# The masks of a dense attention: from matmuls in the sum of scores to transposed masks that multiply the exponentials

## The chip, the cores and the metric

The kernel runs on one core of one Trainium2 chip. The metric is the device time of one execution in microseconds (us), taken without the profiler; a profile of one further execution stands beside it. Times of the kernel before: 1467.72, 1467.99 and 1475.14 us, median 1467.99 us.

## The reference, cut to what matters

Two layers follow one another, each a graph attention and a mixture of experts, on 2708 nodes with 256 features. The change touches the first attention alone. The second attention uses the same adjacency matrix.

```python
# x: (2708, 256) float32; adj: (2708, 2708) int32, zeros and ones
def _L0_gnn_ref(x, adj, Wq, bq, Wk, bk, Wv, bv):
    q = x @ Wq.T + bq
    k = x @ Wk.T + bk
    v = x @ Wv.T + bv
    scores = q @ k.T / jnp.sqrt(jnp.asarray(d, q.dtype))      # d = 256
    neg = jnp.asarray(-9000000000000000.0, scores.dtype)
    scores = jnp.where(adj > 0, scores, neg)
    attention = jax.nn.softmax(scores, axis=-1)
    return jax.nn.elu(attention @ v)
...
x = x + _L0_gnn_ref(_layernorm(x, axis=-1), adj, ...)
x = x + _L0_ffn_ref(_layernorm(x, axis=-1)[None], ...)[0]     # 8 experts, top 2, hidden 1024
x = x + _L1_gnn_ref(_layernorm(x, axis=-1), adj, ...)         # masked by adj too
x = x + _L1_ffn_ref(_layernorm(x, axis=-1)[None], ...)[0]     # 8 experts, top 2, hidden 512
```

A weight of a masked pair is zero after the softmax. So it is the same to push its score far down before the exponential or to multiply its exponential by zero after it.

## The kernel before

Queries go in blocks of 512 (five full blocks and one of 148), keys in 22 tiles of 128 (`NT = 22`; the last has 20 rows). For each block and each key tile `k` there is one step: `scores` makes the sums with the keys on the partitions and the queries along the row, then exponentials `p`; `attend` multiplies `p` of two steps earlier (`LAG = 2`) with `v` into accumulators that live for the whole block.

Rows of `adj` have the queries on the partitions, so a mask lies the wrong way round for the sums. The kernel before turns it with TensorE: `apart` holds 1 where there is no edge, and a matmul of `apart` with -32768 times the identity adds -32768 to the sums of masked pairs. VectorE then reads the mask, turned, back from the sums (`mT`), and each block's `mT` is written to device memory (`neighbours`), from where the second attention takes it.

```python
def load_mask(b, i, into):                       # one of four column quarters of a block's adj
    q = N // 4                                   # 677
    for j, t in enumerate(BLOCKS[b][2]):         # the block's tiles of 128 queries
        r = ROWS[t]
        adj = wide.tile([P, q], I32, name="adj", bufs=4)
        nc.sync.dma_start(adj[:r], a["adj"][t * P : t * P + r, i * q : (i + 1) * q])
        nc.vector.tensor_scalar(
            into[:r, j, i * q : (i + 1) * q], adj[:r], 0, None, ALU.is_le, saturate=False,
        )                                                                    # L255
        yield
...
def scores(b, k, g, apart, mT):
    b0, nb, ts_ = BLOCKS[b]
    kr, k0 = ROWS[k], k * P
    ps = ps_s.tile([P, BN], F32, name="s")                                   # two buffers
    for c in range(DC):                                                      # DC = 2
        nc.tensor.matmul(ps[:kr, :nb], xnT[:, c, k0 : k0 + kr], g[:, c, :nb],
                         start=(c == 0), stop=False)                         # L339
    for j, t in enumerate(ts_):
        r = ROWS[t]
        nc.tensor.matmul(ps[:kr, j * P : j * P + r], apart[:, j, k0 : k0 + kr],
                         minus_big[:, :r], start=False, stop=(j == len(ts_) - 1))   # L345
    p = of_block(b, "p", [P, nb], F32, bufs=4)
    nc.scalar.activation(p[:kr, :nb], ps[:kr, :nb], AF.Exp, scale=1.0 / 16.0)       # L350
    nc.vector.tensor_scalar(mT[:kr, k, :], ps[:kr, :nb], -BIG / 2, None, ALU.is_gt,
                            saturate=False)                                  # L351
    return p

def attend(b, k, p, accs):
    kr = ROWS[k]
    for j, t in enumerate(BLOCKS[b][2]):
        r = ROWS[t]
        nc.tensor.matmul(accs[j][:r], p[:kr, j * P : j * P + r], v[:kr, k, :],
                         start=(k == 0), stop=(k == NT - 1))                 # L361
...
for b, (b0, nb, ts_) in enumerate(BLOCKS):
    mT = of_block(b, "mT", [P, NT, nb], FP8)
    ...
        later_mask = (x for i in range(4) for x in load_mask(b + 1, i, apart_next))
    for k in range(NT):
        ...                                      # block 0: x tiles, its own masks, prepare()
        late.append((b, k, scores(b, k, g, apart, mT)))
        if len(late) > LAG:
            b_, k_, p = late.pop(0)
            ...
            attend(b_, k_, p, accs)
        ...
        if k >= 2:
            next(later_mask, None)               # one piece of the next block's mask per step
        if b > 0:
            if k % 5 == 1 and background:
                background.pop(0)()              # pack one expert's weights, DRAM to DRAM (L587 ...)
            line.step()                          # routing of finished query tiles (L666 ... L731)
        ...
    nc.sync.dma_start(neighbours[b][:], mT)      # L441
```

`adj`, `apart`, `p` and `mT` come from pools with a fixed number of buffers (4 for `adj` and `p`, 2 for `apart` and `mT`). The order of instructions on SyncE's queue is that of the program; it issues the loads, the packing of weights and the stores of the routing.

Of the kernel before, what the change touches and what calls it, by code (L numbers as in the profile page):

```python
# [10 lines left out]
I32 = mybir.dt.int32  # L11
FP8 = mybir.dt.float8e4
U32 = mybir.dt.uint32
BF16 = mybir.dt.bfloat16
AF = mybir.ActivationFunctionType
ALU = mybir.AluOpType
# [3 lines left out]
P = 128  # L20
N = 2708
D = 256
DC = D // P
# [3 lines left out]
NT = (N + P - 1) // P  # L27
# [6 lines left out]
GROUP = 4  # L34
BIG = 32768.0
LAG = 2
# [17 lines left out]
def adj_ffn_kernel(ctx: ExitStack, tc: tile.TileContext, a: dict, out: bass.AP):  # L54
    nc = tc.nc
# [14 lines left out]
    nc.gpsimd.memset(minus_half, -0.5)  # L70

    minus_big = const.tile([P, P], BF16, name="minus_big")
    nc.vector.tensor_scalar(minus_big, ident, -BIG, None, ALU.mult)

# [147 lines left out]
    def layer0_attention(line):  # L222
        with ExitStack() as scope, ExitStack() as until_last:
# [18 lines left out]
            def load_x(t):  # L242
                xin[t] = rows.tile([P, D], F32, name="xin", bufs=9)
                nc.sync.dma_start(xin[t][: ROWS[t]], a["x"][t * P : t * P + ROWS[t], :])

            def load_mask(b, i, into):

                q = N // 4
                for j, t in enumerate(BLOCKS[b][2]):
                    r = ROWS[t]  # L250
                    adj = wide.tile([P, q], I32, name="adj", bufs=4)
                    nc.sync.dma_start(
                        adj[:r], a["adj"][t * P : t * P + r, i * q : (i + 1) * q]
                    )
                    nc.vector.tensor_scalar(  # L255
                        into[:r, j, i * q : (i + 1) * q], adj[:r], 0, None, ALU.is_le,
                        saturate=False,
                    )
                    yield

            def mask_of(b):
                n = len(BLOCKS[b][2])
                apart = of_block(b, "apart", [P, n, N], FP8)
                for j, t in enumerate(BLOCKS[b][2]):
                    if ROWS[t] < P:
                        nc.gpsimd.memset(apart[:, j, :], 0.0)
                return apart

# [3 lines left out]
            with tc.tile_pool(name="fold", bufs=1, side="right") as fold:  # L272
                wq = load_dmajor(fold, "L0_gnn_Wq", D)
                wk = load_dmajor(fold, "L0_gnn_Wk", D)
                apart = mask_of(0)
                for _ in load_mask(0, 0, apart):
                    pass
# [55 lines left out]

            def scores(b, k, g, apart, mT):
                b0, nb, ts_ = BLOCKS[b]
                kr, k0 = ROWS[k], k * P
                ps = ps_s.tile([P, BN], F32, name="s")
                for c in range(DC):
                    nc.tensor.matmul(  # L339
                        ps[:kr, :nb], xnT[:, c, k0 : k0 + kr], g[:, c, :nb],  # L340
                        start=(c == 0), stop=False,
                    )
                for j, t in enumerate(ts_):
                    r = ROWS[t]
                    nc.tensor.matmul(  # L345
                        ps[:kr, j * P : j * P + r], apart[:, j, k0 : k0 + kr], minus_big[:, :r],
                        start=False, stop=(j == len(ts_) - 1),
                    )
                p = of_block(b, "p", [P, nb], F32, bufs=4)
                nc.scalar.activation(p[:kr, :nb], ps[:kr, :nb], AF.Exp, scale=1.0 / 16.0)  # L350
                nc.vector.tensor_scalar(  # L351
                    mT[:kr, k, :], ps[:kr, :nb], -BIG / 2, None, ALU.is_gt,
                    saturate=False,
                )
                return p
# [39 lines left out]
            for b, (b0, nb, ts_) in enumerate(BLOCKS):  # L395
                mT = of_block(b, "mT", [P, NT, nb], FP8)
                nc.gpsimd.memset(mT[:, NT - 1, :], 0.0)
                later_mask = iter(())
                if b + 1 < len(BLOCKS):
                    apart_next = mask_of(b + 1)  # L400
                    later_mask = (x for i in range(4) for x in load_mask(b + 1, i, apart_next))
                for k in range(NT):
                    if b == 0:
                        if k + 6 < NT:
                            load_x(k + 6)
                        if k % 5 == 0 and k < 15:
                            for _ in load_mask(0, k // 5 + 1, apart):
                                pass
                        if k + 4 < NT:
                            prepare(k + 4)  # L410

                    j = k - (2 if b == last else NT - 1 - GROUP)
                    if 0 <= j < len(ts_):
                        load_x(ts_[j])
                    late.append((b, k, scores(b, k, g, apart, mT)))
                    if len(late) > LAG:
# [22 lines left out]
                    if b == last and k == LAG + 2:  # L439
                        experts0.begin()  # L440
                nc.sync.dma_start(neighbours[b][:], mT)  # L441
                if b < last:
                    for _ in later_mask:
                        pass
                    g, apart = g_next, apart_next
            for b_, k_, p in late:
# [536 lines left out]
    for xd in (xd0, xd1):  # L983
        nc.sync.dma_start(xd[N:, :], nobody[:, :D])

    neighbours = [
        dram.tile([P, NT, nb], FP8, name=f"neighbours{b}") for b, (_, nb, _) in enumerate(BLOCKS)
    ]
    line = Line(3)
    layer0_attention(line)  # L990
    with tc.tile_pool(name="mask", bufs=1) as mp:
        mTs = [
            mp.tile([P, NT, nb], FP8, name=f"mT{b}") for b, (_, nb, _) in enumerate(BLOCKS)
        ]
# [45 lines left out]
```

## Time and profile before

| | |
|---|---|
| median time | 1467.99 us |
| span of the profiled execution | 1466.9 us |
| TensorE matmul busy | 1319.2 us (90%) |
| VectorE busy | 574.3 us (39%) |
| ScalarE busy | 371.6 us (25%) |
| GpSimd busy | 449.8 us (31%) |
| moved by DMA | 201.56 MB, mean 137 GB/s |
| first attention, first scores to last product with v | 32.7 to about 557 us |

In the profile PE is TensorE's matmuls, PEld its loads of stationary operands, DVE VectorE, ACT ScalarE, POOL GpSimd, and SPq the queue of SyncE. A row of the groups names the line, the engine, the operation, output<-inputs by the program's names, the shape and the count; behind the bar stand busy time in us, the mean of one in ns, and the idle time of the engine just before them with what ended it. A row of the waits names who waited for whom, the sum in us, how often, and the longest. An fp32 matmul of the program stands as two instructions in the profile.

### The profile page before, as it was taken

The page shows a single profiled execution, that of the slowest core. Times are in us where ns is not written, and L with a number is a line of the kernel's source. Part 1 is how long each engine was busy: PE and PEld are TensorE (multiplying, and loading weights), DVE is VectorE, ACT ScalarE, POOL GpSimd, SP SyncE. Part 2 cuts the span into 40 slices and gives each one's busy share as a digit, 9 for nine tenths or more (in the row PEclk, how much of TensorE's full clock was granted, in tenths as well). Part 3 has the DMA queues.
Part 4 walks back from the last instruction along what each step waited for, and adds up shares of the span by engine and source line. Part 5 has one row for each costly group of instructions (what it writes and reads, how often), then busy time and mean ns, then how long its engine had stood idle before and what let it go on. Part 6 is the DMA issues. An engine that isn't in the chain of part 4 may idle for free. (4 is left out here: it accounts for less than half of the span.)

```text
span 1466.9 us, 22111 instructions
## 1 busy us (share of the span) xinstructions
PE 1319.2 (90%) x7932; PEld 1034.9 (71%) x7932; DVE 574.3 (39%) x2208; ACT 371.6 (25%) x1083; POOL 449.8 (31%) x485
## 2 busy tenths in 40 slices
PE   5999999899899998999999999699899696888882
PEld 3676656566566667999999999577788475777761
DVE  6624634526436255322222222365565463232320
ACT  2222212112122125433333333233011052222220
POOL 5100210101101123433333333331343355455552
PEclk9999999999999999999999999899999897999996
DMA  7603986939532063656686452310111527546464
GB/s 249 196 4 90 254 210 180 249 92 248 139 89 71 35 243 107 193 169 196 203 302 196 107 154 35 69 38 11 63 66 38 209 79 174 133 88 150 92 180 97
DMA packets 109770, 201.56 MB, mean 137 GB/s; under 512 B 25708, under 2 KB 85268, under 8 KB 103340
## 3 DMA queue, kind: packets, MB, share of 16 engines
q1 hardware_dynamic: 76316, 107.99, 26.3%
q0 software_dynamic: 33344, 92.16, 22.6%
q8 instruction: 63, 1.03, 0.3%
q14 instruction: 47, 0.39, 0.1%
HBM read 263.63 MB, written 70.20 MB: 228 GB/s over the span
## 5 line engine op out<-in xcount | busy, mean ns | idle before, releaser
L914 PE MATMUL mm<-xe,ring 128*128 128x128 f32 x2400 | 304.0, 281 | 17.1 <-DMA ring<-L_ffn_packed,weight_row 15.2
L914 PEld LDWEIGHTS mm<-xe,ring 128*128 128x128 f32 x2400 | 292.3, 196 | 35.1 <-issue 25.9
L930 PE MATMUL acc<-ring,hT 128*128 128x256 f32 x1200 | 300.2, 385 | 10.8 <-ACT hT L922 10.8
L922 ACT ACTIVATE hT<-mm,ring 128x128 f32<-128x128 f32 x600 | 171.7, 369 | 397.8 <-issue 283.4
L930 PEld LDWEIGHTS acc<-ring,hT 128*128 128x128 f32 x1200 | 212.5, 191 | 38.3 <-ACT hT L922 17.8
L938 POOL DMA_INDIRECT xd<-y,xg x100 | 159.2, 1592 | 206.0 <-DVE y L936 72.8
L361 PE MATMUL acc<-v,p 128*128 128x257 f32 (+1 forms) x880 | 215.8, 388 | 0.0
L339 PE MATMUL s<-g,xnT 128*128 128x512 f32 (+1 forms) x440 | 214.2, 603 | 0.1
L936 DVE TENSOR_TENSOR y<-acc,bias 128x256 f32<-128x256 f32 x100 | 42.5, 425 | 377.5 <-PE acc L930 306.9
L508 PE MATMUL acc<-parts,mT 128*128 128x257 bf16 (+1 forms) x1452 | 179.5, 277 | 1.9 <-POOL parts L495 1.9
L361 PEld LDWEIGHTS acc<-v,p 128*128 128x128 f32 (+1 forms) x880 | 158.8, 190 | 18.9
L508 PEld LDWEIGHTS <-mT 128*128 128x128 fp8e4 (+1 forms) x1452 | 138.3, 99 | 32.7 <-issue 10.7
L731 POOL DMA_INDIRECT disp<-row,to x88 | 88.3, 1003 | 207.0 <-DVE to L728 110.9
L855 POOL DMA_INDIRECT ring<-L_ffn_packed,weight_row x100 | 105.6, 1056 | 143.9 <-issue 106.3
L154 POOL TENSOR_TENSOR ln_rs<-ln_rs,minus_half 128x2 f32<-128x2 f32 x88 | 66.9, 767 | 269.6 <-DVE ln_rs L150 213.4
L351 DVE TENSOR_SCALAR mT<-s 128x512 fp8e4<-128x512 f32 x110 | 75.7, 688 | 165.8 <-ACT p L350 165.7
L350 ACT ACTIVATE p<-s 128x512 f32<-128x512 f32 x110 | 65.4, 594 | 191.5 <-PE s L345 189.9
L339 PEld LDWEIGHTS s<-g,xnT 128*128 128x128 f32 (+1 forms) x440 | 75.9, 186 | 52.6 <-issue 46.9
L345 PEld LDWEIGHTS <-apart 128*128 128x128 fp8e4 (+1 forms) x440 | 34.0, 98 | 63.9 <-issue 63.9
L255 DVE TENSOR_SCALAR apart<-adj 128x677 fp8e4<-128x677 int32 x80 | 40.0, 511 | 42.6 <-DMA adj<-in_adj_dram 42.3
L894 PE MATMUL tp<-ident,xg 128*128 128x128 f32 x200 | 40.3, 282 | 15.0 <-DMA xg<-disp 13.8
L894 PEld LDWEIGHTS tp<-ident,xg 128*128 128x128 f32 x200 | 28.3, 148 | 23.9 <-issue 16.1
(182 smaller groups left out, 1075.8 us busy)
## 6 DMA issues: line engine op xcount, KB each, us to landing
adj<-in_adj_dram SPq DMA_DIRECT2D x84, 338.5 KB
L_ffn_packed<-in_L_ffn_W_dram SPq DMA_DIRECT2D x16, 1024.0 KB
xg<-disp SPq DMA_DIRECT2D x100, 129.0 KB
L_ffn_packed<-in_L_ffn_W_dram SPq DMA_DIRECT2D x16, 512.0 KB
neighbours<-mT SPq DMA_DIRECT2D x5, 1408.0 KB
mT<-neighbours SPq DMA_DIRECT2D x5, 1408.0 KB
xin<-in_x_dram SPq DMA_DIRECT2D x42, 128.0 KB
xd<-x SPq DMA_DIRECT2D x42, 128.0 KB
```

What stands on the lines that cost most here:

```text
L154: nc.gpsimd.tensor_tensor(rs[:r, 1], rs[:r, 0], minus_half[:r], ALU.pow)
L339: nc.tensor.matmul(ps[:kr, :nb], xnT[:, c, k0 : k0 + kr], g[:, c, :nb], start=(c == 0), stop=False,)
L351: nc.vector.tensor_scalar(mT[:kr, k, :], ps[:kr, :nb], -BIG / 2, None, ALU.is_gt, saturate=False,)
L361: nc.tensor.matmul(accs[j][:r], p[:kr, j * P : j * P + r], v[:kr, k, :], start=(k == 0), stop=(k == NT - 1),)
L508: nc.tensor.matmul(acc[:r], mT[:, k, q0 : q0 + r], parts[:, k, i], start=(k == 0 and i == 0), stop=(k == NT - 1 and i == 2),)
L731: nc.gpsimd.indirect_dma_start(disp[:], bass.IndirectOffsetOnAxis(ap=to[:r, j : j + 1], axis=0), rows2[j][:r], None,)
L855: nc.gpsimd.indirect_dma_start(w, None, packed[:], bass.IndirectOffsetOnAxis(ap=self.weight_row[:, s : s + 1], axis=0), bounds_check=E * P ...
L894: nc.tensor.transpose(tp[:, c, :], xg[:, c * P : (c + 1) * P], ident)
L914: nc.tensor.matmul(ps[:, i, :], w[:, c * hidden + f * P : c * hidden + (f + 1) * P], xe[:, c, :], start=(c == 0), stop=(c == DC - 1),)
L922: nc.scalar.activation(hT[:, f, :], ps[:, i, :], AF.Gelu, bias=w[:, b1 + f : b1 + f + 1])
L930: nc.tensor.matmul(ps, hT[:, f, :], w[:, w2 + f * D : w2 + (f + 1) * D], start=(f == 0), stop=(f == hc - 1),)
L938: nc.gpsimd.indirect_dma_start(xd[:], bass.IndirectOffsetOnAxis(ap=xg.bitcast(I32)[:, D : D + 1], axis=0), y, None, compute_op=ALU.add,)
```

## The change

The mask is turned by transposing transfers instead of TensorE. `adj` is converted by VectorE to bf16 ones and zeros, queries on the partitions (`near`), and `dma_start_transpose` writes it into `mT`, keys on the partitions. The sums keep only the two products of scores; `p` is multiplied with `mT` on VectorE after the exponential. The column quarters become parts of 6, 6, 5 and 5 key tiles, so that each transpose moves whole tiles of 128 columns. `mT` is bf16 and comes from the transposes, no longer from the sums; it is written to `neighbours` in fp8 by a converting transfer that GpSimd issues. It is meant to free TensorE of the mask matmuls.

```diff
-BIG = 32768.0
+
+COLUMNS = [-(-nb // 32) * 32 for _, nb, _ in BLOCKS]
+
+PARTS = [(0, 6), (6, 6), (12, 5), (17, 5)]
...
-    minus_big = const.tile([P, P], BF16, name="minus_big")
-    nc.vector.tensor_scalar(minus_big, ident, -BIG, None, ALU.mult)
...
+            near_end = [pool.tile([P, 5 * P], BF16, name=f"near_end{i}") for i in range(GROUP)]
+            for near in near_end:
+                nc.gpsimd.memset(near, 0.0)
+
             def load_mask(b, i, into):
 
-                q = N // 4
+
+                t0, n = PARTS[i]
+                q0, q1 = t0 * P, min((t0 + n) * P, N)
+                turns = []
                 for j, t in enumerate(BLOCKS[b][2]):
                     r = ROWS[t]
-                    adj = wide.tile([P, q], I32, name="adj", bufs=4)
-                    nc.sync.dma_start(
-                        adj[:r], a["adj"][t * P : t * P + r, i * q : (i + 1) * q]
-                    )
+                    adj = wide.tile([P, 6 * P], I32, name="adj", bufs=4)
+                    nc.sync.dma_start(adj[:r, : q1 - q0], a["adj"][t * P : t * P + r, q0:q1])
+                    if i == len(PARTS) - 1:
+                        near = near_end[j]
+                    else:
+                        near = wide.tile([P, 6 * P], BF16, name="near", bufs=3)
+                    full = -(-r // 32) * 32
+                    if r < P:
+                        nc.gpsimd.memset(near[:full, : n * P], 0.0)
                     nc.vector.tensor_scalar(
-                        into[:r, j, i * q : (i + 1) * q], adj[:r], 0, None, ALU.is_le,
-                        saturate=False,
-                    )
+                        near[:r, : q1 - q0], adj[:r, : q1 - q0], 0, None, ALU.is_gt
+                    )
+                    turns.append((
+                        into[:, t0 : t0 + n, j * P : j * P + full], near[:full, : n * P]
+                    ))
+                    if len(turns) > 2:
+                        nc.sync.dma_start_transpose(*turns.pop(0))
                     yield
+                for turn in turns:
+                    nc.sync.dma_start_transpose(*turn)
 
             def mask_of(b):
-                n = len(BLOCKS[b][2])
-                apart = of_block(b, "apart", [P, n, N], FP8)
-                for j, t in enumerate(BLOCKS[b][2]):
-                    if ROWS[t] < P:
-                        nc.gpsimd.memset(apart[:, j, :], 0.0)
-                return apart
+                return of_block(b, "mT", [P, NT, COLUMNS[b]], BF16)
...
-            def scores(b, k, g, apart, mT):
-                b0, nb, ts_ = BLOCKS[b]
+            def scores(b, k, g, mT):
+                nb = BLOCKS[b][1]
                 kr, k0 = ROWS[k], k * P
                 ps = ps_s.tile([P, BN], F32, name="s")
                 for c in range(DC):
                     nc.tensor.matmul(
                         ps[:kr, :nb], xnT[:, c, k0 : k0 + kr], g[:, c, :nb],
-                        start=(c == 0), stop=False,
-                    )
-                for j, t in enumerate(ts_):
-                    r = ROWS[t]
-                    nc.tensor.matmul(
-                        ps[:kr, j * P : j * P + r], apart[:, j, k0 : k0 + kr], minus_big[:, :r],
-                        start=False, stop=(j == len(ts_) - 1),
+                        start=(c == 0), stop=(c == DC - 1),
                     )
                 p = of_block(b, "p", [P, nb], F32, bufs=4)
                 nc.scalar.activation(p[:kr, :nb], ps[:kr, :nb], AF.Exp, scale=1.0 / 16.0)
-                nc.vector.tensor_scalar(
-                    mT[:kr, k, :], ps[:kr, :nb], -BIG / 2, None, ALU.is_gt,
-                    saturate=False,
-                )
+                nc.vector.tensor_mul(p[:kr, :nb], p[:kr, :nb], mT[:kr, k, :nb])
                 return p
...
-                mT = of_block(b, "mT", [P, NT, nb], FP8)
-                nc.gpsimd.memset(mT[:, NT - 1, :], 0.0)
                 later_mask = iter(())
                 if b + 1 < len(BLOCKS):
-                    apart_next = mask_of(b + 1)
-                    later_mask = (x for i in range(4) for x in load_mask(b + 1, i, apart_next))
+                    mT_next = mask_of(b + 1)
+                    later_mask = (x for i in range(4) for x in load_mask(b + 1, i, mT_next))
...
-                nc.sync.dma_start(neighbours[b][:], mT)
+                nc.gpsimd.dma_start(neighbours[b][:], mT)
...
     neighbours = [
-        dram.tile([P, NT, nb], FP8, name=f"neighbours{b}") for b, (_, nb, _) in enumerate(BLOCKS)
+        dram.tile([P, NT, n], FP8, name=f"neighbours{b}") for b, n in enumerate(COLUMNS)
     ]
```

The rest of the diff passes `mT` where `apart` went, and gives the second attention's copies of `mT` the same widths (160 columns instead of 148 in the last block).

## The prediction

> **What bounds the kernel now.** I read the page first (busy tenths of each engine), then the groups by line inside the first attention, then the order of time on TensorE, and last the waits. The first attention runs from about 33 us to 556 us. The page's tenths say who is full there; the first fourteen or so digits of each row are this stage.
>
> ```profile
> PE   5999999899899998999999999699899696888882
> DVE  6624634526436255322222222365565463232320
> DMA  7603986939532063656686452310111527546464
> ```
>
> TensorE has 9 in nearly every slice, VectorE 2 to 6, and the DMA engines swing between 0 and 9. So TensorE is the engine to shorten, VectorE has room on average, and DMA is busy in bursts. The groups of TensorE between 160 and 520 us show what it does there:
>
> ```profile
> L361 PE MATMUL acc<-v,p 128*128 128x257 f32 (+1 forms) x672 | 164.9, 388 | 0.0
> L339 PE MATMUL s<-g,xnT 128*128 128x512 f32 (+1 forms) x328 | 158.2, 605 | 0.1
> L345 PE MATMUL s<-minus_big,apart 128*128 128x128 bf16 (+1 forms) x328 | 31.9, 220 | 0.0
> ...
> L713 PE MATMUL misc<-sel,before 128*128 128x8 bf16 x16 | 2.8, 176 | 16.8 <-DVE sel L710 16.8
> ```
>
> L345 is what the change takes out. Its mean of 220 ns would make four of them cost 880 ns, and its 31.9 us of busy time over 82 steps (328 matmuls, four to a step) would make it 389 ns a step. Neither is the price, because matmuls overlap: a duration runs from entry to the last result, while the next one is already streaming. The price is the distance from the first mask matmul's start to the start of what follows. The order of time on TensorE gives it:
>
> ```profile
> 422.50 1.88 PE L339 MATMUL s<-g,xnT 128*128 128x512 f32 x4
> 424.21 0.39 PE L345 MATMUL s<-minus_big,apart 128*128 128x128 bf16 x4
> 424.44 1.95 PE L361 MATMUL acc<-v,p 128*128 128x257 f32 x8
> 426.23 1.88 PE L339 MATMUL s<-g,xnT 128*128 128x512 f32 x4
> ```
>
> Start to start: scores 1.71 us, masks 0.23 us, products with v 1.79 us, together 3.73 us a step of one 128-key tile. Over all of the stage I took the same distance wherever a group of four masks is followed by L361: 107 cases, mean 0.232 us, median 0.22 us. In the last block, with two masks a step, it is 0.099 us in 21 cases. TensorE idles before L713 alone (16.8 us in ten waits, for the router's selection on VectorE), so what is taken from its stream comes off the end unless something else begins to hold it.
>
> The waits from 40 to 560 us show what VectorE and the SyncE queue meet:
>
> ```profile
> ACT p L350 <- PE s L345: 188.4, 90, 4.1
> DVE mT L351 <- ACT p L350: 165.7, 63, 6.9
> ...
> DVE apart L255 <- DMA adj<-in_adj_dram: 41.4, 21, 8.2
> ```
>
> ```profile
> SPq L441 <- DVE mT L351: 210.5, 5, 60.8
> ...
> SPq L252 <- DMA L_ffn_packed<-in_L_ffn_W_dram: 29.3, 10, 5.0
> ```
>
> The exponential waits for scores and VectorE waits for the exponential: both are fed by TensorE. But VectorE, which works in order, already stands up to 8.2 us before an adjacency quarter that has not landed, and TensorE did not idle for it. And SyncE's queue stands 210.5 us at the write of neighbours (L441), until a block's last mask is made; then the packings that stood behind it come out in a bunch. The stretches of 20 us show what that does in block 1, which begins near 142 us (columns: length, busy time and count of PE, PEld, DVE, ACT, POOL, clock, DMA share, GB/s):
>
> ```profile
> 142.00:160.00 18.00, 18.00 (x80) 12.14 (x81) 15.25 (x55) 5.13 (x11) 2.55 (x5) 1.00 1.05 271
> 160.00:180.00 20.00, 18.66 (x88) 12.02 (x87) 12.80 (x52) 4.14 (x11) 3.77 (x5) 1.00 1.04 250
> 180.00:200.00 20.00, 18.44 (x85) 12.20 (x84) 7.11 (x24) 3.31 (x8) 3.28 (x5) 1.00 1.05 247
> ...
> 220.00:240.00 20.00, 20.00 (x86) 12.54 (x84) 4.57 (x8) 3.36 (x7) 0.53 (x1) 1.00 0.36 122
> ```
>
> For 58 us of a block of some 83 us the DMA engines are full, at about 255 GB/s; then they are nearly free.
>
> **What the Trainium skill says.** "VectorE: DVE Perf Modes", section "The TRN2 errata", gives (N+151)/0.96 ns for an fp32 tensor_tensor, 691 ns at N = 512. This trace agrees within 3% at 256 columns: L380, a 128x256 fp32 sum of two tiles in SBUF, has a mean of 414 ns where the formula gives 424. The same page, "The three transpose paths", has one 128x128 bf16 transpose by DMA at 1309 ns. "DMA: Bandwidth & Descriptors", section "Latency and other measured facts", has 261 GB/s for DMA transposes with a non-contiguous middle dimension, which is the shape here. No transposing transfer is in this trace, so neither figure can be checked yet. That page's "Queues, rings and completion order" says that each DMA engine takes the descriptors of one queue in ring order. The trace fits: an adjacency load issued at 159.44 us, behind a weight packing issued from 152.99 us on, was waited for by VectorE until 168.28 us, 8.8 us later.
>
> **The change part by part.**
>
> *TensorE, removed.* 110 steps of four masks x 0.232 us = 25.5 us, and 22 steps of two x 0.099 us = 2.2 us: 27.7 us in all, or 1.9%. That is the ceiling of the direct gain; 2% would be 29.4 us.
>
> *VectorE, exchanged.* The test of the sums that made mT (L351, 688 ns, 110 times) goes; a product of p and mT comes, an estimate of 691 ns from the VectorE page. The conversion of adj stays, 677 columns in 511 ns now; with the same fixed 151 cycles and two elements a cycle the formula gives 510 for it, and 557, 491 and 434 ns for the new parts of 768, 640 and 532 columns. VectorE's sum does not move by more than a few us.
>
> *The chain to the products with v.* Before, p was ready after the exponential (594 ns). Now it needs 0.69 us more. Attend runs two steps late: between the end of scores k and attend k stand attend k-2, scores k+1, attend k-1 and scores k+2, 1.79 + 1.71 + 1.79 + 1.71 = 7.0 us. Exponential and product take 1.3 us, so 5.7 us are left for VectorE to be late in.
>
> *Transfers added.* 16 transposes in each full block, 128 x 768 or 128 x 640 bf16: a block's mask is 512 x 2816 x 2 bytes = 2.9 MB, and all blocks 15.3 MB. At 261 GB/s (estimate from the DMA page) one takes 0.75 us and a block's take 11 us. The neighbours write now reads 2.9 MB for the 1.4 MB it moved, and is issued by GpSimd: some 6 us more at 255 GB/s. Block 1's 58 full us become about 75, which just fits in a block of 22 steps at 3.5 us, 77 us and its routing. In return SyncE loses its 210.5 us of standing, and can issue packings and loads of the next block earlier.
>
> *New waits.* A transpose stands in SyncE's queue until its conversion is done, and the next quarter's first adj load is issued behind the last transpose of this quarter. Before, loads were ahead by four buffers; at each quarter's edge the lead falls to one step. From a conversion's end: two issues of transposes (under 1.5 us each by the 1309 ns), one load (from 20.04 us to 23.05 us in the trace, 3.0 us), so near 5 us against a step of 3.5 us. VectorE stands about 1.5 us at each edge, inside the 5.7 us. Behind a packing a load took 8.8 us, so with the two transposes' issues VectorE stands 6 to 7 us where an edge and a packing meet, past the limit by about 1 us. There are 16 packings, all in blocks 1 to 4, and on full DMA engines the transposes wait as well; I put 12 us for these stalls, three quarters of a us for each packing. The ten waits of L713 for VectorE do not shrink with TensorE's step: 10 x 0.23 = 2 us kept.
>
> Sum: 1468.0 - 27.7 + 12 + 2 = 1454 us. The start (four clears of near_end on GpSimd against those of mT and apart that go) I take as even. I predict 1454 us.
>
> **The rivals.**
>
> *A, the full 28 us or a little more.* For it: 41.4 us of adj waits on VectorE cost TensorE nothing before, PSUM is now released by the exponential instead of VectorE's later pass, and SyncE no longer stands at L441. Against it: the longer series of load, conversion, transpose and product. It gives 1438 to 1441 us.
>
> *B, transposes in series.* If six 128x128 blocks follow one another at 1309 ns, a transpose takes 7.9 us and 16 take over 115 us, while a block of 22 steps takes 22 x 3.5 = 77 us on TensorE. With three near buffers the conversion waits for the transpose three before it, VectorE stands, and the product with it: 30 to 40 us for each of four or five blocks, 1570 to 1630 us. For it: SyncE issues every transpose, and no row of this trace shows how fast one is. Against it: 261 GB/s on the DMA page, and a 1309 ns that is mostly one transfer's latency. A milder form, 3 to 4 us each, ties the transposes to TensorE's step and gives 1470 to 1510 us.
>
> *C, full DMA engines take the gain.* The 75 us of DMA are reckoned, not seen; if they are 90, the masks of the next block come as slowly as DMA allows, VectorE stands in order before its conversions, and blocks 1 to 3, which hold 15 of the packings, stretch to the DMA's length, 5 to 10 us each. That returns 15 to 30 us: 1457 to 1472 us. For it: the share of 1.05 above. Against it: the smoother issue, and 20 us of nearly free DMA late in block 1.
>
> **Range and chances.** The centre lies between A and C. The lower end, 1436 us, is A with 4 us from the smoother queue; the upper, 1500 us, takes in C and most of the milder B. More than 2% faster needs below 1438.6 us, beyond the direct saving: 0.13. Within 2% (up to 1497.3 us): 0.67. Slower by more, which is B: 0.20.
>
> **What would show it.** No L345 row, and L361 starting 1.7 us after scores: the removal. A product row near 690 ns: VectorE as reckoned. The step of TensorE at 3.5 us where no routing runs; if it stays near 3.7 us, with products with v waiting for p, and the DMA share at 1 through blocks 1 to 3, C. Transposes landing within about 4 us of issue; if VectorE's conversions wait long for them, B. TensorE's idle time before L361, zero now, is the number that tells all three apart. I am wrong if the saving of a step is not 0.23 us, or if the transposes' speed, which no trace here gives, is far from the estimate.

## The result, and the profile after

The changed kernel takes 1532.36 us (median of 4; 1528.95 to 1534.61) against 1468.53 us beside it: a ratio of 1.042 (95% interval 1.039 to 1.046), 64 us slower. The profiled execution has a span of 1529.5 us.

The page's tenths, after, for the same three engines and the granted clock of TensorE:

```profile
PE   5968979677877999999999999969998795898882
DVE  3443631531632725532222222255546544222321
PEclk9988999798998999999999999979999899999996
DMA  7786599899696313465668653220111517545564
```

The first attention now fills some sixteen digits instead of fifteen. TensorE falls to 6 and 7 in it, its clock to 7 and 8, and DMA is at 5 to 8 in the first five slices, where it had a 0 and a 3 before, and at 8 and 9 in the next five. VectorE is no busier, but it stands longer (it waits, and everything behind it in its order waits too), as the groups show (line, engine, operation, count, then busy us, mean ns, idle time before it and what ended it):

```profile
L366 PE MATMUL acc<-v,p 128*128 128x257 f32 (+1 forms) x880 | 222.9, 398 | 58.7 <-DVE p L359 42.1
...
L353 PE MATMUL s<-g,xnT 128*128 128x512 f32 (+1 forms) x440 | 223.3, 625 | 0.0
...
L359 DVE TENSOR_TENSOR p<-p,mT 128x512 f32<-128x512 f32 x110 | 75.0, 685 | 73.8 <-ACT p L358 71.6
L268 DVE TENSOR_SCALAR near<-adj 128x768 bf16<-128x768 int32 (+1 forms) x66 | 35.3, 535 | 155.9 <-DMA adj<-in_adj_dram 149.3
```

The mask matmuls are gone. The products with v, which had no idle time before them, now wait 58.7 us: 42.1 us for the product of p and mask on VectorE, and most of the rest in a single wait that is told below. The product of p and mask takes 685 ns, as reckoned. The conversions of adj stand 149.3 us before loads. The waits from 40 to 640 us add those of the last parts (`near_end`) and name the longest:

```profile
DVE near L268 <- DMA adj<-in_adj_dram: 144.4, 26, 21.4
...
DVE near_end L268 <- DMA adj<-in_adj_dram: 43.8, 13, 11.7
...
PE acc L366 <- DVE p L359: 42.1, 8, 12.8
...
PE misc L716 <- DVE sel L713: 34.3, 12, 6.6
```

VectorE stood 41.4 us before loads of adj (8.2 us at most); now 188.2 us, 21.4 us at most. TensorE's waits from 30 to 622 us make up all of its idle time in the stage, 92.3 us; before, only those for `sel`, the routing's choice of experts, were there (16.8 us):

```profile
PE acc L366 <- DVE p L359: 42.1, 8, 12.8
PE misc L716 <- DVE sel L713: 33.0, 11, 6.6
PE acc L366 <- DVE raw L391: 16.5, 1, 16.5
PE misc L164 <- DVE xn L158: 0.7, 3, 0.3
```

Where that becomes idle time of TensorE is plain at the end of block 0. VectorE in order of time:

```profile
119.39 0.69 DVE L359 TENSOR_TENSOR p<-p,mT 128x512 f32<-128x512 f32 x1 [1.52 <-ACT p L358]
140.09 0.56 DVE L268 TENSOR_SCALAR near<-adj 128x768 bf16<-128x768 int32 x1 [20.01 <-DMA adj<-in_adj_dram]
141.02 0.56 DVE L268 TENSOR_SCALAR near<-adj 128x768 bf16<-128x768 int32 x1 [0.36 <-DMA adj<-in_adj_dram]
141.50 0.69 DVE L359 TENSOR_TENSOR p<-p,mT 128x512 f32<-128x512 f32 x1
```

and TensorE:

```profile
133.30 1.88 PE L353 MATMUL s<-g,xnT 128*128 128x512 f32 x4
142.24 3.79 PE L366 MATMUL acc<-v,p 128*128 128x257 f32 x8 [7.05 <-DVE p L359]
```

The conversions at 140 us are of block 2's mask, needed more than 100 us later; the products behind them are of block 0, needed at once. VectorE takes them in this fixed order, so TensorE waits for a load that it does not need. In the program's text the conversion stands in block 1; the scheduler that orders all engines but SyncE set it ahead of six products of block 0. Its load left SyncE at 131.58 us, behind the first packing of weights (118.92 us). In the kernel before, the first conversion of block 2 stands in block 1, where the text has it:

```profile
152.07 0.52 DVE L255 TENSOR_SCALAR apart<-adj 128x677 fp8e4<-128x677 int32 x1 [0.71 <-DMA adj<-in_adj_dram]
```

The other block edges look alike: the first conversions of blocks 3, 4 and 5 wait 21.4, 19.9 and 20.2 us. At the edge from block 1 to block 2 it is not a product that is late but two copies (`raw`) that empty the accumulators of block 1. They stand behind the first conversion of block 3, and TensorE can't go on with block 2's products with v until they are done:

```profile
279.41 0.56 DVE L268 TENSOR_SCALAR near<-adj 128x768 bf16<-128x768 int32 x1 [21.36 <-DMA adj<-in_adj_dram]
...
280.49 0.75 DVE L391 COPY raw<-acc 128x257 f32<-128x257 f32 x2
```

```profile
280.96 2.94 PE L366 MATMUL acc<-v,p 128*128 128x257 f32 x6 [16.55 <-DVE raw L391]
```

This is the longest of all TensorE's waits in the stage.

Cut at ScalarE's last copy out of the accumulators of each block (columns as in the prediction; the wait of 16.55 us falls into block 2), blocks 0, 2 and 4 before and after:

```profile
32.70:143.87 111.17, 111.15 (x489) 73.69 (x488) 46.12 (x98) 29.57 (x65) 8.97 (x12) 1.00 0.31 100
...
240.18:335.19 95.01, 89.79 (x393) 57.70 (x393) 43.08 (x154) 19.03 (x42) 12.16 (x17) 1.00 0.76 190
...
430.29:516.42 86.13, 84.33 (x389) 56.77 (x390) 39.41 (x148) 17.73 (x43) 11.49 (x16) 1.00 0.23 66
```

```profile
32.60:165.74 133.14, 111.33 (x393) 70.89 (x392) 50.83 (x117) 29.53 (x65) 13.36 (x17) 0.92 0.67 161
...
262.11:393.33 131.22, 92.27 (x305) 57.55 (x306) 44.46 (x158) 19.13 (x43) 12.33 (x17) 0.84 0.85 179
...
503.75:584.52 80.77, 78.56 (x305) 52.63 (x306) 39.51 (x146) 17.92 (x43) 14.40 (x19) 1.00 0.23 60
```

Block 4 has only a small mask to load beside it, and is 5.4 us shorter: 22 x 0.232 us is 5.1. Blocks 0 and 2 are 22 and 36 us longer, with 22 and 39 us of TensorE idle. And block 2 is granted a clock of 0.84: fewer matmuls (305 records for 393) cost more busy time, 92.27 us for 89.79.

The sum over the stage, from the first scores to the last product with v: 523.8 us before, 588.6 us after. Idle time of TensorE went from 16.9 to 92.3 us (+75.4), its busy time from 506.9 to 496.3 us (-10.6): +64.8 us. Outside the stage nothing moved (943.1 and 940.9 us).

### The profile page after: what moved, and what is told of

The parts are those of the page before. It is cut to its first block, busy times and chain, and to the rows that moved or that the text cites. A ratio compares the mean times of both kernels' runs of the same rounds, so it can differ in the third digit from the quotient of the medians.

```text
span 1529.5 us, 21244 instructions
## 1 busy us (share of the span) xinstructions
PE 1312.8 (86%) x7448; PEld 1022.4 (67%) x7448; DVE 572.7 (37%) x2207; ACT 368.9 (24%) x1081; POOL 454.5 (30%) x492
## 5 line engine op out<-in xcount | busy, mean ns | idle before, releaser
L366 PE MATMUL acc<-v,p 128*128 128x257 f32 (+1 forms) x880 | 222.9, 398 | 58.7 <-DVE p L359 42.1
L366 PEld LDWEIGHTS acc<-v,p 128*128 128x128 f32 (+1 forms) x880 | 174.1, 200 | 140.8 <-DVE p L359 50.7
L933 PEld LDWEIGHTS acc<-ring,hT 128*128 128x128 f32 x1200 | 212.7, 192 | 37.4 <-ACT hT L925 16.8
L353 PE MATMUL s<-g,xnT 128*128 128x512 f32 (+1 forms) x440 | 223.3, 625 | 0.0
L359 DVE TENSOR_TENSOR p<-p,mT 128x512 f32<-128x512 f32 x110 | 75.0, 685 | 73.8 <-ACT p L358 71.6
L268 DVE TENSOR_SCALAR near<-adj 128x768 bf16<-128x768 int32 (+1 forms) x66 | 35.3, 535 | 155.9 <-DMA adj<-in_adj_dram 149.3
L897 PE MATMUL tp<-ident,xg 128*128 128x128 f32 x200 | 40.2, 278 | 17.2 <-DMA xg<-disp 16.5
L716 PE MATMUL misc<-sel,before 128*128 128x8 bf16 x44 | 7.8, 177 | 52.4 <-DVE sel L713 51.5
L703 ACT ACTIVATE p<-p 128x2 f32<-128x2 f32 (+3 forms) x44 | 9.1, 206 | 153.7 <-DVE p L702 141.0
```

The costliest lines, as they stand in the source:

```text
L359: nc.vector.tensor_mul(p[:kr, :nb], p[:kr, :nb], mT[:kr, k, :nb])
L933: nc.tensor.matmul(ps, hT[:, f, :], w[:, w2 + f * D : w2 + (f + 1) * D], start=(f == 0), stop=(f == hc - 1),)
```

## The experiments

All runs, with the stage, TensorE's idle time in it and in blocks 0 to 3, and DMA time in the stage (share times length). A time is the median of the executions without profile, with their number. "Order", "later", "x" and "packs" are the four mends told below. Executions of one kernel on one chip differ by up to 16 us (1469.52 to 1485.24 us for the kernel before beside e13 to e16), and chips differ too. The kernel before took 1469.68 us beside e1, e2, e4 and e6 (one execution), 1470.71 beside e9 to e12, 1476.10 beside e13 to e16 and 1471.68 beside e17 and e18; ratios are to these. In "changed" and e8 one wait of TensorE at the edge of blocks 1 and 2 (16.5 and 22.3 us) is counted in block 2.

| run | time us (n) | stage us | PE idle us | blocks 0/1/2/3 | DMA us |
|---|---|---|---|---|---|
| before | 1467.99 (3) | 523.8 | 16.9 | 0/5/5/5 | 290 |
| changed | 1532.36 (4) | 588.6 | 92.3 | 22/8/39/21 | 416 |
| e1 before, no mask matmuls | 1450.39 (1) | 499.5 | 21.7 | 0/7/6/7 | 288 |
| e4 before, transposes added | 1480.21 (1) | 538.5 | 22.8 | 1/5/6/8 | 397 |
| e6 no transposes | 1483.27 (1) | 516.4 | 32.9 | 7/7/6/13 | 297 |
| e2 VectorE in program order | 1559.58 (1) | 573.2 | 71.0 | 19/10/22/12 | 409 |
| e3 converting loads | 1493.97 (1) | 550.6 | 60.9 | 27/4/20/8 | 436 |
| e5 SyncE held | 1518.99 (1) | 573.4 | 76.0 | 17/14/23/18 | 434 |
| e7 order | 1520.34 (1) | 568.6 | 77.7 | 17/11/31/16 | 426 |
| e8 later | 1516.55 (1) | 568.5 | 79.3 | 17/5/42/13 | 423 |
| e9 packs | 1516.77 (2) | 564.5 | 74.2 | 21/19/17/15 | 388 |
| e10 before, packs | 1474.66 (10) | 524.6 | 16.1 | 0/5/6/5 | 272 |
| e11 converting loads, x, packs | 1498.20 (2) | 553.4 | 62.8 | 31/9/9/8 | 411 |
| e12 order, later, x, packs | 1448.41 (2) | 501.8 | 24.2 | 3/1/11/8 | 390 |
| e13 later, x, packs | 1519.60 (2) | 566.7 | 73.5 | 21/18/17/11 | 391 |
| e14 order, x, packs | 1472.78 (18) | 515.4 | 33.0 | 1/3/13/13 | 389 |
| e15 order, later, packs | 1462.80 (18) | 506.4 | 28.6 | 8/1/9/9 | 397 |
| e16 order, later, x | 1451.24 (2) | 502.5 | 27.8 | 1/2/21/3 | 408 |
| e17 as e12, six adj buffers | 1474.08 (12) | 518.3 | 38.5 | 1/7/15/14 | 388 |
| e18 as e12, again | 1449.50 (4) | 496.7 | 21.8 | 0/2/10/9 | 387 |

**e1: the mask matmuls alone.** The masking is left out of the sums.

```diff
-                        start=(c == 0), stop=False,
+                        start=(c == 0), stop=(c == DC - 1),
                     )
-                for j, t in enumerate(ts_):
-                    r = ROWS[t]
-                    nc.tensor.matmul(
-                        ps[:kr, j * P : j * P + r], apart[:, j, k0 : k0 + kr], minus_big[:, :r],
-                        start=False, stop=(j == len(ts_) - 1),
-                    )
```

> The kernel before without the mask matmuls; loads, conversions, the test of the sums and all else stay, so attention is over all pairs (the masking is left out). If a step of TensorE is shorter by the 0.23 us read from the order of time, about 1440 us (1468 less 27.7). If the mask matmuls were partly hidden, 1450 to 1468 us.

The stage is 24.3 us shorter, the total 19.3 us. The 27.7 us are there: busy time falls by 29.1 us; 4.8 us come back as idle time and 6.1 us outside the stage. So about 1450 us is what this removal brought here, in one execution, and the changed kernel lost 82 us on top.

**e4: what the transposes cost in DMA time.** A constant tile is transposed 88 times; its result is not used.

```diff
+                    nc.sync.dma_start_transpose(
+                        turned[:, :n, j * P : j * P + full], near[:full, : n * P]
+                    )
                     yield
```

> The kernel before with 88 added transposes of a constant tile into a tile that nobody reads, one behind each load of adj on SyncE's queue; nothing waits for them but later transposes. It shows what they cost in DMA time alone. By the reckoned 0.75 us each: 59 us of DMA time in all and a time within 5 us of 1468 us. If they take about 117 us of DMA time, as the queue's share after the change says, the loads come later: 1470 to 1500 us.

DMA time in the stage rises by 107 us, nearly twice the 59 us reckoned: 1.2 us for one, 143 GB/s for the 15.3 MB. On SyncE one holds the queue for 1.2 us:

```profile
L266 SPq DMA_TRANSPOSE turned<-near x88: 1164/1216/5402, 12.3 to 460.6; - x88
```

Yet the total rises by 10.5 us only, the stage by 15 us, and TensorE's idle time by 6 us. The traffic by itself, even at a DMA share of 1.02 and 0.96 in blocks 1 and 2, is not the loss of 64 us.

**e6: no transposes.** One mask of ones stands for all blocks, so the masking is left out.

```diff
-                        nc.sync.dma_start_transpose(*turns.pop(0))
+                        turns.pop(0)
...
-                for turn in turns:
-                    nc.sync.dma_start_transpose(*turn)
...
-                return of_block(b, "mT", [P, NT, COLUMNS[b]], BF16)
+                return every_mT[:, :, : COLUMNS[b]]
```

> The changed kernel without its 88 transposes; one constant mask of ones stands for all blocks, loads, conversions, products and the write of neighbours stay (so masking is left out). Theory 1 in the form that transposes' traffic and their place in SyncE's queue make the loads late: about 1440 us. If the early packing of weights, which SyncE reaches now because no write of neighbours holds it, makes the loads late by itself: 1480 to 1530 us.

The stage begins 20 us late here, which the edit itself brought (the mask is set once by VectorE at the start), so it is the stage that counts: 516.4 us, 72 us under the changed kernel and 17 us over e1. With the transposes go the waits of SyncE for conversions and of conversions for near; loads come earlier (VectorE stands 60.3 us before those of near, not 144.4). The total of 1483 us lies in the second expected range only through the late start; without those 20 us it would be about 1463 us, between the two. The scheduler sets conversions ahead here too, the first of block 2 behind eleven products of block 0, but the first conversions of blocks 2 to 5 wait only 5.2 to 7.6 us, and TensorE waits 2.3 us in all for products. By this run the order costs much only where the loads are late too, and transposes in SyncE's queue bring most of the loss, but not all.

**e2: VectorE in the program's order.**

```diff
-    ctx.enter_context(tc.manual_schedule(engines={mybir.EngineType.SP}))
+    ctx.enter_context(tc.manual_schedule(engines={mybir.EngineType.SP, mybir.EngineType.DVE}))
```

> The changed kernel with VectorE's instructions in the order of the program instead of the scheduler's, which sets conversions of masks that are needed a block later ahead of products that are needed now. Theory 1 (VectorE stands, in order, before conversions whose loads are late, and the products behind them starve TensorE): most of the 64 us comes back, 1450 to 1490 us, and TensorE's idle time before the products with v falls from 58.7 us to under 20 us. Theory 2 (the DMA engines are simply full and the masks come late whatever the order): 1515 to 1540 us.

27 us slower, against the expectation. The edit was too wide: outside the stage it costs 44 us (984.7 for 940.9 us). Inside, the waits of products with v for VectorE fell from 42.1 us to 12.5 us, and 48.3 us for normed rows (`xn`) took their place.

**e3, e5, e7, e8: four single mends.** The single execution of the kernel before beside these four took 1496.38 us, far above its usual; theirs show 942 to 950 us outside the stage, as elsewhere, so the stage and the idle time are read, and no ratio is formed.

e3 loads near directly as bf16 by converting transfers of GpSimd:

```diff
-                    nc.sync.dma_start(adj[:r, : q1 - q0], a["adj"][t * P : t * P + r, q0:q1])
...
-                    nc.vector.tensor_scalar(
-                        near[:r, : q1 - q0], adj[:r, : q1 - q0], 0, None, ALU.is_gt
-                    )
+                    nc.gpsimd.dma_start(near[:r, : q1 - q0], a["adj"][t * P : t * P + r, q0:q1])
```

> The changed kernel with near loaded straight as bf16 by converting transfers that GpSimd issues: no adj tile, no conversion on VectorE; transposes and products stay. If VectorE's standing before late loads is what starves TensorE: PE idle in blocks 0 to 3 falls from 90 us towards 25 us, and 1460 to 1490 us. If the masks themselves arrive too late because DMA is full in blocks 1 to 3: 1515 us or more, with products waiting for mT.

The stage is 38 us shorter than in the changed kernel, and the total lies between the two expected ranges. VectorE no longer stands before adj, but 56.5 us before x loads of block 0, which share SyncE's queue with the transposes, and DMA is at 1.08 in block 2.

e5 holds SyncE at each block's end, as the write of neighbours did:

```diff
                 nc.gpsimd.dma_start(neighbours[b][:], mT)
+                nc.sync.dma_start(held[b], late[-1][2][:1, :1])
```

> The changed kernel with SyncE held at each block's end by a store of one element of the block's last p, where the write of neighbours held it before. If it is the packings and loads issued a block too early that hurt (the 20 us wait of VectorE at 120 to 140 us for a load of block 2, behind a packing): block 0 loses its 22 us of PE idle time and the total is 1490 to 1515 us. If being held only pushes transfers later into full blocks: 1530 us or slower.

15 us of the stage come back: TensorE's idle time falls from 47 to 37 us in blocks 1 and 2 together, and block 0 keeps 17 of its 22 us. The run changes two things at once: loads are issued later, and the scheduler set the first conversions of blocks 2 to 5 back into the block where the text has them (block 2's waits 4.5 us instead of 20.0, block 3's still 15.9). So it does not tell early issue from order.

e7 ("order") keeps each conversion behind the product of its own step; `products` collects the products:

```diff
+                    if products:
+                        tc.add_manual_dep(
+                            turned.ins, products[-1].ins.name,
+                            mybir.DependencyInfo(
+                                mybir.DependencyClass.NoSync, mybir.DependencyReason.DATA
+                            ),
+                            reason="behind the product of its step",
+                        )
```

> The changed kernel in the scheduler's order but for one thing: each conversion of a mask is kept behind the product of its own step. Order theory: 1490 to 1515 us, PE idle before the products with v from 58.7 to under 25 us, without the time that the whole order of the program cost outside the stage in the run of that order (28 us slower than the changed kernel, though its stage was 15 us shorter). If the standing is the same wherever the conversions sit: 1525 to 1540 us.

The mechanism shows, and the gain hardly does (20 us of the stage). Products with v wait for VectorE's products 0.7 us in all, for 42.1. But VectorE still stands 120.7 us before loads, and now what is behind the conversions is the routing (`sel`, 33.9 us) and the normed rows (33.3 us), for which TensorE waits instead.

e8 ("later") issues transposes five conversions late, over the edges of quarters, with six near buffers:

```diff
-                        near = wide.tile([P, 6 * P], BF16, name="near", bufs=3)
+                        near = wide.tile([P, 6 * P], BF16, name="near", bufs=6)
...
-                    if len(turns) > 2:
+                    if len(turns) > (2 if b == 0 else 5):
...
-                for turn in turns:
-                    nc.sync.dma_start_transpose(*turn)
+                while turns and (b == 0 or i == len(PARTS) - 1):
+                    nc.sync.dma_start_transpose(*turns.pop(0))
```

> The changed kernel with transposes issued five conversions later and six near buffers (three before), across the edges of quarters for blocks 1 to 5: loads get their lead of four buffers back, the traffic stays. If the lost lead is the cause: 1480 to 1505 us. If the order on VectorE or the DMA time is: 1520 to 1535 us.

20 us of the stage come back; blocks 0, 1 and 3 are better, block 2 is not (42 us idle): VectorE stands 29.9 us before the first load of block 3, and TensorE 22.3 us for the copies behind it. By itself the lost lead is not the cause either.

**e9, e10: thinner packing ("packs"), in the changed kernel and, as control, in the one before.**

```diff
-                        if k % 5 == 1 and background:
+                        if k % 10 == 1 and background:
```

> The changed kernel with the packing of expert weights at every tenth step instead of every fifth, so blocks 1 to 3 carry three packings each instead of five, and blocks 4 and 5 take the rest. If full DMA engines in blocks 1 to 3 are a necessary part of the loss: 1480 to 1500 us, with the PE idle time of blocks 1 to 3 from 68 us to under 35 us and block 0 as slow as it was. If the chain of load, conversion, transpose and product stands by itself: 1520 us or more.

> The kernel before with the same thinner packing, as a control. Its DMA engines have time left, so both theories expect 1463 to 1470 us.

e9: ratio 1.029 (1.026 to 1.032), between the two expected ranges and close to the second. DMA shares in blocks 1 to 3 fall to 0.71 to 0.79 and the idle time there is still 51 us. So full DMA engines are not needed for the loss. The control is 1.002 (1.0004 to 1.0043), so thinner packing by itself gains nothing.

**e11, e12: mends together.** Both add "x": in block 0 the x loads are issued by ScalarE.

```diff
-                            load_x(k + 6)
+                            load_x(k + 6, nc.scalar)
```

> Converting loads instead of VectorE's conversions (the best run so far, 1494 us), the thinner packing, and in block 0 the x loads issued by ScalarE so that they do not stand behind transposes in SyncE's queue. If the remaining loss of 1494 us is x loads in block 0 and full DMA engines in blocks 2 and 3: 1450 to 1468 us, at or below the kernel before. If converting loads are themselves too dear in DMA time (436 us in the stage): 1475 us or more.

> The changed kernel with conversions behind their step's product, transposes five conversions later, x loads of block 0 issued by ScalarE, and the thinner packing. Each of the first two gave back 12 to 16 us alone. If lateness has no other source: 1445 to 1475 us. If conversions on VectorE must stand before loads as long as loads, transposes and packings share one queue: 1480 us or more.

e11 stays at 1498 us (1487.88 and 1508.53): GpSimd, which now issues the loads, is late with the factors of the norms (VectorE waits 84.1 us for them, up to 30.5 us). e12 takes 1448.41 us, ratio 0.983 (0.978 to 0.988), with all 88 transposes in it; e18 is the same kernel again, 1449.50 us, ratio 0.984 (0.979 to 0.988). That is e1's time, with the masking in: all that the removal brought there. "Order", "later" and "x" were not run apart from the change; "x" acts in block 0, where the kernel before has no idle time of TensorE to lose.

**e13 to e16: all mends but one.**

> The run with all four mends (1448 us) without the first: the scheduler again sets conversions ahead of products. If the standing of VectorE before late loads is decisive: 1490 us or more, with PE idle before the products with v. If the other three make the loads early enough: under 1460 us.

> All mends but the later transposes (three near buffers, transposes at most two conversions late, the edge of each quarter drained). If the lost lead of the loads at quarter edges is decisive: 1480 us or more. If it is hidden once conversions stand behind products: under 1460 us.

> All mends but the x loads by ScalarE: in block 0 x tiles stand in SyncE's queue behind transposes again. If that is decisive for block 0: block 0 from 109 us to 120 us or more, total 1460 to 1470 us; blocks 1 to 5 unchanged.

> All mends but the thinner packing: five packings a block in blocks 1 to 3. If full DMA engines are decisive: 1475 us or more, PE idle in blocks 1 to 3 from 20 us to over 40 us. If the chain's order was the cause: under 1460 us.

Without "order" most of the loss is back, 1519.60 us (ratio 1.029; the changed kernel has 1.042); without "later" 1472.78 (1.000), without "x" 1462.80 (0.991), without "packs" 1451.24 us (0.983). Blocks 1 to 3 of e12:

```profile
142.43:226.99 84.56, 83.59 (x305) 53.45 (x306) 43.06 (x154) 19.04 (x43) 14.32 (x17) 1.00 0.89 198
226.99:324.12 97.13, 86.40 (x305) 54.83 (x305) 42.96 (x154) 18.92 (x42) 14.88 (x17) 0.95 0.89 194
324.12:418.44 94.32, 86.25 (x305) 54.94 (x305) 43.01 (x154) 18.93 (x42) 15.69 (x19) 0.95 0.87 197
```

and of e13, where SyncE's and TensorE's instructions stand in the same order as in e12; VectorE's conversions stand elsewhere, and the scheduler set some of ScalarE's and GpSimd's instructions anew around them:

```profile
167.45:272.88 105.43, 87.48 (x305) 55.53 (x305) 42.65 (x154) 19.14 (x42) 13.09 (x17) 0.92 0.83 178
272.88:377.45 104.57, 87.76 (x305) 55.27 (x305) 42.52 (x154) 19.13 (x42) 13.73 (x17) 0.92 0.81 179
377.45:477.04 99.59, 88.67 (x305) 56.09 (x305) 42.51 (x154) 19.14 (x42) 14.11 (x19) 0.93 0.71 164
```

The DMA share of e13 is lower than that of e12, and it is slower: DMA has time, VectorE stands at the wrong place. Its waits in e13, and TensorE's for it:

```profile
DVE near L270 <- DMA adj<-in_adj_dram: 94.6, 20, 19.5
...
PE acc L376 <- DVE p L369: 42.8, 5, 12.7
```

In e12 the first of these is 41.2 us (10 times, 11.7 us at most), and the second is not among its waits of any length. The first conversions of blocks 2 to 5 wait 18.1, 19.5, 16.3 and 15.2 us in e13, ahead of products of the block before the one where the text has them; in e12, in their place, 1.0, 11.7, 10.1 and 1.1 us. That the loss then feeds itself, late products making late steps, late free buffers and late loads, fits these numbers and is not shown apart.

**e17: more buffers for loads.**

```diff
-                    adj = wide.tile([P, 6 * P], I32, name="adj", bufs=4)
+                    adj = wide.tile([P, 6 * P], I32, name="adj", bufs=6)
```

> The run with all four mends and six adj buffers instead of four. SyncE's order is the same; only its waits for free buffers go. If the 47.6 us that VectorE still stands before loads come from loads issued too late for want of buffers: they halve and the total falls by 5 to 10 us below the run with four. If from transfers ahead of them in the queue: within 3 us of it.

Neither expectation held: VectorE stands 44.6 us, hardly less, and the time is 25 us above e18's, 1.001 of the kernel before (0.999 to 1.003). TensorE waits 21.3 us for `sel` (4.8 us in e12). The order of the instructions differs in one place on VectorE alone, a conversion set three instructions earlier in block 0. Why it costs that much is open. So a difference of this size, as between e12 and e14 or e15, is not safely put down to the one mend left out; the 71 us between e12 and e13 are nearly three times as much.

## Why the prediction was wrong, point by point

1454 us were forecast, with a range of 1436 to 1500 us; 1532.36 us were measured. The saving and the cost of VectorE's instructions were right, and the transposes were mis-sized without much harm. The step that failed is the fifth below, the new waits.

- *The mask matmuls, 27.7 us.* Right. e1's busy time falls by 29.1 us, and in the changed kernel blocks 4 and 5, where nothing disturbs, are 5.4 and 3.4 us shorter, for 5.1 and 2.2 reckoned.
- *VectorE's exchange.* Right: a mean of 685 ns for 691, medians of 436 ns for 434 (532 columns) and 552 ns for 557 (768 columns).
- *The chain to the products with v, 5.7 us of room.* Right as a length; what was put into it was wrong.
- *The transposes, 59 us.* Mis-sized: 107 us in e4, 143 GB/s where the Trainium skill's "DMA: Bandwidth & Descriptors", section "Latency and other measured facts", gave 261; the measurement decides. It is not what cost the time, for e12 holds them all at 1448 us. The room for them was misread too, without harm: block 1 of the kernel before is 96 us long (143.87 to 240.18), not the "some 83 us" that its steps alone make.
- *New waits, 12 us.* Here it failed. "VectorE stands about 1.5 us at each edge, inside the 5.7 us", and "6 to 7 us where an edge and a packing meet, past the limit by about 1 us". Two tacit assumptions stood behind it. First, that a conversion stands on VectorE behind the product of its step, as the text has it. It stood ahead, the first of block 2 even before six products of block 0, and e13 against e12 shows that this decides between 1520 and 1448 us once the other mends are in. The kernel before has such an order in block 0 too (block 1's loads are all issued by 60 us, early in the block) at no cost, and e6 has it at the block edges, with waits of 5.2 to 7.6 us, at little cost: what is new is that the loads are late as well. Second, that a late load delays the next load by little. VectorE stood up to 21.4 us, 188 us in all. TensorE's idle time grew by 75.4 us for the 12 + 2 reckoned: 42.1 us before products with v, 16.5 us for the copies out of the accumulators, a way from VectorE to TensorE that the prediction does not have, and 16.2 us more for `sel`.
- *SyncE's freedom from the write of neighbours* was entered as a gain. It let block 1's packing and block 2's loads start in block 0, where the 20 us stand came from; e5 takes it away, together with the order at the block edges, and gets 15 us of the stage back.
- *The clock* had no term. The changed kernel and e12 have the same matmuls; their busy time in the stage is 496.3 and 477.6 us at granted clocks of 0.84 to 0.95 and 0.95 to 1.00 in blocks 1 to 3. That is 19 us more, beside 68 us more idle time (92.3 and 24.2 us). The Trainium skill would have said so: "TensorE: Matmul & The Clock Gate", section "What's actually happening", has the clock halved after an idle window of about 3.4 us and full again after as long a busy one. The trace agrees in direction; around the longest idle stretch, at the edge of blocks 1 and 2, the changed kernel shows

```profile
260.00:280.00 20.00, 4.42 (x15) 2.46 (x14) 0.59 (x2) 1.94 (x4) 0.00 (x0) 0.68 0.99 202
280.00:300.00 20.00, 18.46 (x64) 12.41 (x65) 18.36 (x70) 4.50 (x11) 2.87 (x5) 0.90 0.67 167
```

  15.6 us idle of 20 and a clock of 0.68, then still 0.90.
- *The rivals.* B, slow transposes in series, is false: 1.2 us each; the slow end of the forecast (0.20) stood on it alone. C names the right place, VectorE in order before its conversions, with the wrong cause, and its 15 to 30 us are at most about a third of the 82 us lost: e9 has DMA shares under 0.8 and loses 46 us, e16 has shares of 1.02 and 1.04 in blocks 1 and 2 and takes 1451 us. A, about 1440 us, was not reached by e1 either.

What stays open is which second mend "order" needs at least: alone it gives 1520 us, with any two of the others or all three 1448 to 1473 us; pairs were not run.

## What to carry to other kernels

When work moves onto an engine that also waits for transfers, ask what stands ahead of it in that engine's order, not how busy the engine is: VectorE was 37% busy and starved TensorE. Read the order from the trace or the built program before trusting the text; where a scheduler sets a wait for a far block ahead of work for this one, one ordering edge can be worth more than bandwidth. Here it was worth 20 us of the stage alone and 73 us or more with any two of the other mends (e7; e14, e15, e16), so look for the second wait behind the first. Products are not the only work that can stand behind such a wait: the copies that free accumulators do too. A prediction needs a term for what a stall does to the stalled engine's clock.

## What the hardware showed that was not expected

- A transpose of 128 x 768 or 128 x 640 bf16 within SBUF takes about 1.2 us of all DMA engines (107 us for 88, 143 GB/s), in small packets: e4 has 62,656 more packets than the kernel before, all of them under 512 bytes.
- TensorE's granted clock follows its idle time within a block: 1.00 with 2 us idle in 81 us, 0.92 with 21 in 110, 0.84 with 39 in 131. Against e12, 68 us more idle time went with 19 us more busy time for the same matmuls.
- The write of masks from bf16 to fp8 by GpSimd's queue and the transposes hardly slow TensorE by their traffic: e12 moves 92 MB in a stage in which the kernel before moved 80.5 MB, in 22 us less.
